# Two cross-attention layers in one launch: an own plan for the first seven steps, image tokens in five pieces, ScalarE's projection copies between layer 1's two pairs, image probabilities turned one place later

## The chip, the cores and the metric

The kernel runs on one core of one Trainium2 chip. What is measured is the device time of one execution in microseconds (us). The core has a matrix engine (TensorE, PE in the profile; its weight loads are the row PEld), a vector engine (VectorE, DVE), a scalar engine (ScalarE, ACT), a general engine (GpSimd, POOL) and a sync engine (SP) that issues transfers. Each engine works through its own list of instructions in the order in which the program issued them; semaphores hold an instruction until what it needs is there. Matrix products land in PSUM, and the other engines copy them from there to SBUF.

## What is computed

Eight batch entries of 256 rows and 320 channels go through two attention layers of 20 heads with 16 channels each. Both layers take their keys and values from 256 context tokens of 512 channels. Layer 0 treats the first 77 tokens as text and the other 179 as image tokens, with a softmax for each part. Layer 1 treats 252 as text and the last 4 as image tokens, and adds a term to the image scores: how alike the text context that a row attends to is to each image token.

```python
# layer 0
q = heads(x @ Wq.T); k, v from text; k_ip, v_ip from the rest
out = (softmax(q k / 4) v + softmax(q k_ip / 4) v_ip) @ Wo.T + bo + x
# layer 1, on layer 0's result
probs_t = softmax(q k_t / 4);  text_out = probs_t v_t
qsem = l2norm(probs_t @ text_ehs);  sem = qsem . l2norm(ip_ehs)
probs_ip = softmax(q k_ip / 4 + 0.5 * sem) * spatial_mask
out = (text_out + probs_ip v_ip) @ W_out + b_out + x
```

All numbers are float32. The biases are drawn small and not zero.

## The kernel before

**Steps.** The 20 heads of a batch entry are handled in five groups of four (QUADS), so a layer takes 40 steps. The loop at L910 walks n from 0: step n does group s = n % 5 of entry b = n // 5 for layer 0, and beside it the group of layer 1 that lies six steps back (SHIFT). The first six steps have no layer 1 in them, 34 steps have both layers, and at the end six steps have layer 1 alone; four more only drain. Nothing is reordered by a scheduler: manual_schedule keeps PE, DVE, ACT and POOL in the order in which the Python code issues the instructions.

**One step of both layers** (both_layers, L853). Scores of layer 0 go to four PSUM tiles (one for each head, held once each, so the next scores wait until these are emptied). DVE takes the row maxima (l0_max, L411, which run at L414), ACT the exponentials with their sums (l0_exp, L422, at L426), in two pairs of heads. PE turns each pair (transposed_probs, L349, at L357) into the same PSUM tiles, DVE and ACT copy the turned probabilities out (L362), and at the end of the step PE multiplies them with the values (l0_values, at L444). Between, layer 1 does the same: scores at L319, maxima and exponentials in max_exp1 (L849, at L614 and L626), the turning at L357, and, one step later, the products y with values and gram matrix (l1_values, L650 and L653), which DVE reduces (L657, L661). POOL prepares the masked queries sc_qz (L308) that the scores of either layer wait for.

**Fillers.** Everything else is put into seven places (0 to 6) of a step by a table in fillers (L778): projections to q, k and v of both layers (l0_q, l0_k, l0_v, l1_q, l1_k, l1_v), the gram matrix (l1_gram), output projections, layer 1's end (l1_norm to l1_out). A filler of this kind takes one of two PSUM tiles (mm_tile, L92), PE writes it, and ACT or DVE copies it out: ACT at L258 (q), L390 (k of layer 0), L399 and L401 (v of layer 0), L501 and L502 (k of layer 1), L536 (gram), L554 and L555 (v of layer 1). A third filler can't begin on PE before the first one's copy has been made. One place in the plan brings l1_k at place 4 (0, 4) and l1_xT at place 5 (0, 5), which turns layer 0's result for layer 1 (L287, with two such tiles). l1_probs_T (L708) turns layer 1's image probabilities on PE (L712), scales the text part on POOL (L721) and copies on DVE (L729); it stands in place 3 of group 3, ahead of layer 1's scores. l1_attn uses it in place 5.

**The first steps.** Steps 0 to 3 (n < NQ - 1) have a plan of their own; steps 4 to 6 use the general one. image_tokens (L209) prepares the 32 image tokens of all entries at once, at place 4 of step 1: turning them (L213, copied at L216), their keys (ps_kip, 24 products at L220), their values (L281, copied at L230), the squares on ACT (L233), their root on ACT (L235, with a table load, since the exponential's table must give way), the scaling on DVE (L236, L237), and turning the scaled tokens (L240, L243). Their source ip_sb comes by eight small transfers that POOL issues behind three weights (load_late, L759). encT and xT of entry 1 are issued on ACT's queue at step 2.

Of the kernel before, what the change touches and what calls it, by code (L numbers as in the profile page):

```python
# [50 lines left out]
def kernel(  # L51
# [40 lines left out]
    def mm_tile(name):  # L92
        return ps_mm.tile([P, 512], F32, tag="mm", name=name)
# [115 lines left out]
    def image_tokens(_):  # L209
        ipT = work.tile([P, NE, NB], F32, tag="aT", name="ipT", bufs=2)  # L210
        ps = mm_tile("ps_ipT")
        for k in range(NE):
            nc.tensor.transpose(  # L213
                ps[:, k * NB : (k + 1) * NB], ip_sb[:, k * P : (k + 1) * P], ident[:NB, :NB]
            )
        nc.vector.tensor_copy(ipT.rearrange("p k n -> p (k n)"), ps[:, : NE * NB])  # L216
        ps = mm_tile("ps_kip")
        for m in range(NC):
            for k in range(NE):
                nc.tensor.matmul(  # L220
                    ps[:, m * NB : (m + 1) * NB],
                    columns(wkip1, k, m),
                    ipT[:, k, :],
                    start=(k == 0),
                    stop=(k == NE - 1),
                )
        nc.vector.tensor_copy(kipA.rearrange("p m n -> p (m n)"), ps[:, : NC * NB])
        ps = mm_tile("ps_vip")
        project_rows(ps[:NB, :C], lambda k: ipT[:, k, :], wvip1)
        nc.vector.tensor_copy(vipA, ps[:NB, :C])  # L230
        sq = work.tile([NB, E], F32, tag="et1", name="ip_sq", bufs=2)
        rn = small.tile([NB, 1], F32, tag="ip_rn", name="ip_rn", bufs=1)
        nc.scalar.activation(sq, ip_sb, AF.Square, accum_out=rn)  # L233
        nc.vector.tensor_scalar_max(rn, rn, EPS2)
        nc.scalar.activation(rn, rn, AF.Sqrt)  # L235
        nc.vector.reciprocal(rn, rn)  # L236
        nc.vector.tensor_scalar_mul(sq, ip_sb, rn)  # L237
        ps = mm_tile("ps_ip")
        for k in range(NE):
            nc.tensor.transpose(  # L240
                ps[:, k * NB : (k + 1) * NB], sq[:, k * P : (k + 1) * P], ident[:NB, :NB]
            )
        nc.vector.tensor_copy(ipnT.rearrange("p k n -> p (k n)"), ps[:, : NE * NB])  # L243


    def project_q(dst, src, w, ms, name):
# [531 lines left out]
    def fillers(n, place):  # L778
# [45 lines left out]
        for f, at, *args in plan.get((s, place), ()):  # L824
            if 0 <= at < B:
                f(at, *args)
# [19 lines left out]

        return l1_begin(*divmod(n - SHIFT, NQ), 1 if n < N0 else n % 2)

    def max_exp1(u, x):  # L849
        l1_max(u, x)  # L850
        l1_exp(u, x)

    def both_layers(n, u, v1):  # L853

        u0 = l0_begin(*divmod(n, NQ))
        for pair in range(2):
            l0_max(u0, pair)
        l0_exp(u0, 0)
        fillers(n, 0)
        part(l1_values, v1, 0)  # L860
        l0_exp(u0, 1)
        fillers(n, 1)
        part(l0_attn, u)
# [12 lines left out]
        part(l1_values, v1, 3, (0,))  # L876
        part(l1_transposed, u1, 0)
        fillers(n, 5)
        part(l1_values, v1, 3, (1,))
        part(l1_transposed, u1, 1)  # L880
        fillers(n, 6)
        l0_values(u0)
        return u0, u1

    def layer_1(n, u, v1):

        fillers(n, 0)
        fillers(n, 1)
        part(l0_attn, u)
        u1 = begin1(n)  # L890
        part(max_exp1, u1, 0)
        part(l1_values, v1, 0)
        fillers(n, 2)
        part(max_exp1, u1, 1)
# [86 lines left out]
```

## Time and profile before

Three executions were timed, 943.75, 944.04 and 948.78 us, so the median is 944.04. The execution that was profiled took 944.11 us.

| | us |
|---|---|
| profiled execution | 944.11 |
| its span in the trace | 942.4 |
| outside the span | 1.7 |
| PE busy | 893.2 (95%) |
| PEld busy | 715.4 (76%) |
| DVE busy | 626.4 (66%) |
| ACT busy | 530.8 (56%) |
| POOL busy | 199.3 (21%) |
| mean granted TensorE clock | 0.987 |

A step begins with its scores of layer 0 (L319 on PE). Read so, the first seven steps lie as follows. The columns are the stretch, its length, PE's busy time in it and the mean granted clock of PE.

| step | from, to (us) | length | PE busy | clock |
|---|---|---|---|---|
| 0 | 13.80 to 25.01 | 11.21 | 11.21 | 1.00 |
| 1 | 25.01 to 46.16 | 21.15 | 17.23 | 0.84 |
| 2 | 46.16 to 59.04 | 12.88 | 12.88 | 0.87 |
| 3 | 59.04 to 72.46 | 13.42 | 12.48 | 1.00 |
| 4 | 72.46 to 85.80 | 13.34 | 10.83 | 0.87 |
| 5 | 85.80 to 105.44 | 19.64 | 17.55 | 1.00 |
| 6 | 105.44 to 122.63 | 17.19 | 15.81 | 1.00 |

In a timeline a row gives the start, the time from the first instruction's start to the last one's end, the engine, the line, the operation and the tiles, how many instructions are merged, and in brackets the idle time ahead of it with what ended it. A matmul's row overlaps the next by some 0.1 us. In the table of waits a row names who waited, for whom, how long in total, how often, and the longest.

### The profile page before, as it was taken

How to read it: one execution, taken by the hardware profiler on the slowest of the kernel's cores; microseconds unless marked ns; L12 is line 12 of the kernel's file. 1: busy time of each engine (PE TensorE's matmuls, PEld its weight loads, DVE VectorE, ACT ScalarE, POOL GpSimd, SP SyncE). 2: the span in 40 equal slices, each digit the busy share in tenths (PEclk: the TensorE clock that was granted, in tenths of full speed). 3: DMA queues.
4: the chain of work that ended last, by engine and by line, in shares of the span. 5: the costliest groups of instructions: out<-in, count | busy, mean ns of one | idle time of the engine just before them, and what ended most of it. 6: DMA issues, size and time to landing. Idle time of an engine off the chain costs nothing.

```text
span 942.4 us, 18840 instructions
## 1 busy us (share of the span) xinstructions
PE 893.2 (95%) x6296; PEld 715.4 (76%) x6296; DVE 626.4 (66%) x2127; ACT 530.8 (56%) x2314; POOL 199.3 (21%) x336
## 2 busy tenths in 40 slices
PE   7898999999999999999999999999999999899895
PEld 5576687878877787878787788777877787768773
DVE  2344466767776677766777667766777667875774
ACT  3476465746645576545666467555665556643650
POOL 5422221123121222122121221312221122212100
PEclk9899999999999999999999999999999999999997
DMA  8310010001000010000100001000100100000000
GB/s 267 99 46 1 15 41 1 1 15 36 9 2 15 16 44 2 15 16 23 23 1 15 15 24 22 2 15 15 44 2 8 26 2 1 1 15 1 1 15 15
DMA packets 16848, 21.89 MB, mean 23 GB/s; under 512 B 1632, under 2 KB 15904, under 8 KB 16752
## 3 DMA queue, kind: packets, MB, share of 16 engines
q1 hardware_dynamic: 12048, 12.49, 5.1%
q0 software_dynamic: 1296, 4.25, 1.5%
q10 hardware_dynamic: 3408, 3.95, 1.3%
q8 instruction: 51, 0.84, 0.4%
q14 instruction: 45, 0.37, 0.1%
HBM read 17.24 MB, written 2.62 MB: 21 GB/s over the span
## 4 chain that ended last, share of the span: by engine, by line
PE 66%; issue 15%; ACT 9%; DVE 5%; POOL 3%; DMA 1%; ACTq 0%; POOLq 0%; DVEq 0%
PE y L650 11%; PE sc L357 10%; PE sc L319 8%; PE v L281 6%; PE k L269 6%; PE p_o L294 6%; PE y L653 6%; PE q L251 5%; ACT e L626 5%; PE oT L444 4%; ACT e L426 4%; DVE nmx L614 2%; POOL sc_qz L308 2%; PE g L527 2%; PE p_aT_ps L287 1%
## 5 line engine op out<-in xcount | busy, mean ns | idle before, releaser
L426 ACT ACTIVATE e<-sc,nmx 128x77 f32<-128x77 f32 (+1 forms) x640 | 228.0, 416 | 58.2 <-DVE nmx L414 58.2
L626 ACT ACTIVATE e<-sc,nmx 128x252 f32<-128x252 f32 x320 | 145.8, 479 | 124.3 <-DVE aip L617 120.7
L650 PE MATMUL y<-gv,et 126*128 126x272 f32 x640 | 201.6, 396 | 3.8 <-DVE num L661 3.7
L357 PE MATMUL sc<-ident,e 128*126 128x128 f32 (+1 forms) x1280 | 171.3, 275 | 12.8 <-ACT e L426 7.3
L657 DVE CUSTOM_DVE_ANT_0 e<-y,e 128x252 f32<-128x252 f32 x320 | 133.6, 418 | 71.6 <-PE y L653 69.2
L414 DVE TENSOR_REDUCE nmx<-sc 128x2 f32<-128x154 f32 x320 | 109.7, 415 | 102.0 <-PE sc L319 102.0
L362 DVE COPY et<-sc 128x512 f32<-128x512 f32 (+1 forms) x228 | 151.2, 687 | 17.2 <-PE sc L357 14.4
L426 ACT ACTIVATION_READ_ACCUMULATOR e<-sc,nmx 128x1 f32 x640 | 162.2, 254 | 0.0
L357 PEld LDWEIGHTS sc<-ident,e 128*126 128x126 f32 (+1 forms) x1280 | 145.3, 141 | 22.0 <-ACT e L426 10.6
L653 PEld LDWEIGHTS y<-gv,et 126*128 126x128 f32 x640 | 120.8, 189 | 25.8
L653 PE MATMUL y<-gv,et 126*128 126x146 f32 x640 | 131.4, 287 | 0.0
L614 DVE TENSOR_REDUCE nmx<-sc 128x2 f32<-128x504 f32 x160 | 106.8, 675 | 29.3 <-PE sc L319 29.3
L650 PEld LDWEIGHTS y<-gv,et 126*128 126x128 f32 x640 | 104.4, 190 | 18.0 <-issue 4.7
L362 ACT COPY et<-sc 128x512 f32<-128x512 f32 (+1 forms) x92 | 53.2, 585 | 100.8 <-PE sc L357 100.8
L319 PE MATMUL sc<-k,sc_qz 32*128 32x256 f32 x1280 | 94.1, 404 | 2.9 <-POOL sc_qz L308 2.6
L479 POOL TENSOR_TENSOR attn<-o_sb 128x64 f32<-128x64 f32 x80 | 24.0, 321 | 313.3 <-DVE o_sb L469 310.3
L319 PEld LDWEIGHTS sc<-k,sc_qz 32*128 32x128 f32 x1280 | 58.9, 185 | 32.5 <-issue 21.7
L540 POOL COPY gv<-gv 126x3402 f32<-126x3402 f32 (+1 forms) x16 | 33.2, 2077 | 214.3 <-ACT gv L536 162.3
L308 POOL TENSOR_SCALAR sc_qz<-q,quad_m 128x256 f32<-128x256 f32 x80 | 73.2, 925 | 4.2 <-ACT q L258 4.2
L269 PE MATMUL k<-encT,wk 128*128 128x77 f32 (+1 forms) x384 | 72.8, 332 | 0.7 <-DMA wk<-in_WkT_dram 0.7
L269 PEld LDWEIGHTS k<-encT,wk 128*128 128x128 f32 x384 | 58.1, 190 | 16.3 <-issue 12.6
L626 ACT ACTIVATION_READ_ACCUMULATOR e<-sc,nmx 128x1 f32 x320 | 68.4, 214 | 0.0
(129 smaller groups left out, 1070.7 us busy)
## 6 DMA issues: line engine op xcount, KB each, us to landing
encT<-in_encT_dram SPq DMA_DIRECT2D x7, 512.0 KB
x<-in_x_dram SPq DMA_DIRECT2D x8, 320.0 KB
out_dram<-osb SPq DMA_DIRECT2D x16, 160.0 KB
xT<-in_xT_dram SPq DMA_DIRECT2D x7, 256.0 KB
xT<-in_xT_dram SPq DMA_DIRECT2D x7, 128.0 KB
vip_rows<-vipA SPq DMA_DIRECT2D x32, 25.0 KB
wk<-in_WkT_dram ACTq DMA_DIRECT2D x1, 640.0 KB
wkip<-in_WkipT_dram ACTq DMA_DIRECT2D x1, 640.0 KB
```

The costliest lines, as they stand in the source:

```text
L269: nc.tensor.matmul(ps[:, t0:t1], columns(w, k, m), encT_b[:, k, t0:t1], start=(k == 0), stop=(k == NE - 1),)
L308: nc.gpsimd.tensor_scalar_mul(qz, qT[:, m, :], quad_m[:, i : i + 1])
L319: nc.tensor.matmul(sc[j][:, half, :], qz[rows, half * P : (half + 1) * P], kT(j)[rows, m, :], start=True, stop=True,)
L357: nc.tensor.transpose(v[:, c, half, :], u["e"][x][:, j, half, t0 + c * tn : t0 + (c + 1) * tn], ident,)
L362: copies[j](u["et"][x][:tn, j].rearrange("p c n s -> p (c n s)"), ps)
L414: nc.vector.tensor_reduce(u["nmx"][x][:, j, :, a], u["sc"][2 * x + j][:, :, t0:t1], AX.X, ALU.max, negate=True,)
L426: nc.scalar.activation(u["e"][x][:, j, half, t0:t1], u["sc"][2 * x + j][:, half, t0:t1], AF.Exp, bias=u["nmx"][x][:, j, half, a : a + 1], ...
L614: nc.vector.tensor_reduce(u["nmx"][x][:, j, :], sc[:, :, t0 : t0 + TXT1], AX.X, ALU.max, negate=True)
L626: nc.scalar.activation(u["e"][x][:, j, half, t0 : t0 + TXT1], u["sc"][2 * x + j][:, half, t0 : t0 + TXT1], AF.Exp, bias=u["nmx"][x][:, j, ...
L650: nc.tensor.matmul(y, et[:, 1 - odd, half, :], gv[0][:, g, full], start=True, stop=False)
L653: nc.tensor.matmul(y[:, into], et[:, odd, half, :], gv[1][:, g, part], start=False, stop=True)
L657: nc.vector.tensor_tensor_reduce(e, y[:, g0 : g0 + TXT1], e, op0=ALU.mult, op1=ALU.add, scale=1.0, scalar=0.0, accum_out=r["n2"][:, half, ...
```

## The change

Four edits. image_tokens becomes five fillers: ip_squares (the squares and their sum, now one DVE instruction), ip_norm (root on ACT, reciprocal and scaling on DVE), ip_T (turning tokens and scaled tokens together), ip_k and ip_v. They stand in steps 1 and 2. The first seven steps (0 to 6) get one plan of their own; it issues the same fillers as those steps did before, at other places, each keyed by step and place. In both_layers the maxima of both pairs of layer 1 are issued first, then the exponentials of pair 0, then the fillers of place 4, and then the exponentials of pair 1; ACT's copies of place 4 so stand ahead of pair 1's exponentials, where they stood behind them. l1_probs_T moves from place 3 of group 3 to place 4, behind layer 1's scores and ahead of l0_q. In layer_1 max_exp1 is written out, with no change of order.

```diff
+    def ip_squares(_):
+        ip["n"] = work.tile([NB, E], F32, tag="et1", name="ip_n", bufs=2)
+        ip["rn"] = small.tile([NB, 1], F32, tag="ip_rn", name="ip_rn", bufs=1)
+        nc.vector.tensor_tensor_reduce(
+            ip["n"], ip_sb, ip_sb, op0=ALU.mult, op1=ALU.add,
+            scale=1.0, scalar=0.0, accum_out=ip["rn"],
+        )
+        nc.vector.tensor_scalar_max(ip["rn"], ip["rn"], EPS2)
+
+    def ip_norm(_):
+        nc.scalar.activation(ip["rn"], ip["rn"], AF.Sqrt)
+        nc.vector.reciprocal(ip["rn"], ip["rn"])
+        nc.vector.tensor_scalar_mul(ip["n"], ip_sb, ip["rn"])
...
-        nc.scalar.activation(sq, ip_sb, AF.Square, accum_out=rn)
...
-            (3, 3): [(l1_probs_T, old)],
-            (3, 4): [(l0_q, ahead, (0, 1))],
+            (3, 4): [(l1_probs_T, old), (l0_q, ahead, (0, 1))],
...
-        if n < NQ - 1:
-            plan = {
-                (0, 0): [(l0_v, 0, 0)],
-                (0, 1): [(l0_v, 0, 1)],
-                (0, 2): [(l0_v, 0, 2)],
-                (1, 0): [(l0_k, 0, 1)],
-                (1, 1): [(l0_q, 0, (2,))],
-                (1, 4): [(image_tokens, 0)],
-                (2, 0): [(l1_gram, 0, 0)],
-                (2, 1): [(l1_v, 0, 0)],
-                (2, 2): [(l0_k, 0, 2)],
-                (3, 0): [(l1_v, 0, 1)],
-                (3, 1): [(l0_v, 1, 0)],
-                (3, 4): [(l0_q, 1, (0, 1)), (l1_gram, 0, 1), (l1_image, 0)],
-            }
+        if n <= NQ + 1:
+            plan = (
+                {
+                    0: [(l0_v, 0, 0)],
+                    1: [(l0_v, 0, 1)],
+                    2: [(l0_v, 0, 2)],
+                },
+                {
+                    0: [(l0_k, 0, 1)],
+                    1: [(l0_k, 0, 2), (ip_squares, 0)],
+                    2: [(l0_q, 0, (2,)), (ip_norm, 0)],
+                },
+                {
+                    0: [(ip_T, 0), (ip_k, 0)],
+                    1: [(ip_v, 0)],
+                    2: [(l1_gram, 0, 0)],
+                    3: [(l1_v, 0, 0)],
+                },
+                {
+                    0: [(l1_v, 0, 1)],
+                    1: [(l0_q, 1, (0, 1)), (l1_image, 0)],
+                    2: [(l0_v, 1, 0)],
+                },
+                {
+                    0: [(l0_k, 1, 0)],
+                    1: [(l0_v, 1, 1)],
+                    2: [(l1_gram, 0, 1), (l1_k, 0, 0)],
+                },
+                {
+                    0: [(l0_v, 1, 2)],
+                    1: [(l0_k, 1, 1)],
+                    2: [(l0_q, 1, (2,)), (l0_attn_T, 0, 0)],
+                    3: [(l0_attn_T, 0, 1), (l0_out, 0, 0), (l0_out, 0, 1)],
+                    5: [(l1_xT, 0)],
+                    6: [(l1_q, 0, (0, 1))],
+                },
+                {
+                    0: [(l1_k, 0, 2)],
+                    4: [(l1_k, 0, 1)],
+                    5: [(l1_gram, 1, 0)],
+                },
+            )[n]
+            plan = {(s, at): f for at, f in plan.items()}
...
         u1 = begin1(n)
-        part(max_exp1, u1, 0)
-        part(max_exp1, u1, 1)
+        for pair in range(2):
+            part(l1_max, u1, pair)
+        part(l1_exp, u1, 0)
         fillers(n, 4)
+        part(l1_exp, u1, 1)
         part(l1_values, v1, 3, (0,))
         part(l1_transposed, u1, 0)
```

More of the change, by code (lines that the diff above doesn't have):

```diff
@@ L207, with ip_T, ip_k @@
     vipA = const.tile([NB, C], F32, tag="vipA", name="vipA")
-    def image_tokens(_):
-        ipT = work.tile([P, NE, NB], F32, tag="aT", name="ipT", bufs=2)
-        ps = mm_tile("ps_ipT")
-        for k in range(NE):
-            nc.tensor.transpose(
-                ps[:, k * NB : (k + 1) * NB], ip_sb[:, k * P : (k + 1) * P], ident[:NB, :NB]
+    ip = {}
+    def ip_squares(_):
[10 more added lines that the diff above has]
+        nc.vector.tensor_scalar_mul(ip["n"], ip_sb, ip["rn"])
+    def ip_T(_):
+        ip["T"] = work.tile([P, NE, NB], F32, tag="aT", name="ipT", bufs=2)
+        ps = mm_tile("ps_ipT")
+        for i, src in enumerate((ip_sb, ip["n"])):
+            for k in range(NE):
+                nc.tensor.transpose(
+                    ps[:, (i * NE + k) * NB : (i * NE + k + 1) * NB],
+                    src[:, k * P : (k + 1) * P],
+                    ident[:NB, :NB],
+                )
+        for i, dst in enumerate((ip["T"], ipnT)):
+            nc.vector.tensor_copy(
+                dst.rearrange("p k n -> p (k n)"), ps[:, i * NE * NB : (i + 1) * NE * NB]
             )
-        nc.vector.tensor_copy(ipT.rearrange("p k n -> p (k n)"), ps[:, : NE * NB])
+    def ip_k(_):
         ps = mm_tile("ps_kip")
@@ L222, in image_tokens @@
                     columns(wkip1, k, m),
-                    ipT[:, k, :],
+                    ip["T"][:, k, :],
                     start=(k == 0),
@@ L227, in image_tokens, with ip_v @@
         nc.vector.tensor_copy(kipA.rearrange("p m n -> p (m n)"), ps[:, : NC * NB])
+    def ip_v(_):
         ps = mm_tile("ps_vip")
-        project_rows(ps[:NB, :C], lambda k: ipT[:, k, :], wvip1)
+        project_rows(ps[:NB, :C], lambda k: ip["T"][:, k, :], wvip1)
         nc.vector.tensor_copy(vipA, ps[:NB, :C])
-        sq = work.tile([NB, E], F32, tag="et1", name="ip_sq", bufs=2)
-        rn = small.tile([NB, 1], F32, tag="ip_rn", name="ip_rn", bufs=1)
-        nc.scalar.activation(sq, ip_sb, AF.Square, accum_out=rn)
[L234 to L243, printed above, removed]
     def project_q(dst, src, w, ms, name):
@@ L847, in begin1 @@
         return l1_begin(*divmod(n - SHIFT, NQ), 1 if n < N0 else n % 2)
-    def max_exp1(u, x):
-        l1_max(u, x)
-        l1_exp(u, x)
     def both_layers(n, u, v1):
@@ L890, in layer_1 @@
         u1 = begin1(n)
-        part(max_exp1, u1, 0)
+        part(l1_max, u1, 0)
+        part(l1_exp, u1, 0)
         part(l1_values, v1, 0)
         fillers(n, 2)
-        part(max_exp1, u1, 1)
+        part(l1_max, u1, 1)
+        part(l1_exp, u1, 1)
         part(l1_values, v1, 1)
```

## The prediction

> **What bounds the kernel now.** I read the page's slices first, then the table of who waits for whom on PE in the steady part, the chain of waits there, and last the start in one-microsecond windows.
>
> ```profile
> PE   7898999999999999999999999999999999899895
> ...
> PEclk9899999999999999999999999999999999999997
> ```
>
> PE is busy nearly everywhere. Only two things can be won: PE's idle time, and time at a lower granted clock. Both lie in the first five slices (118 us) and at the very end. The steady part, 150 to 800 us:
>
> ```profile
> PE x1T_ps L287 <- ACT k L502: 7.5, 6, 1.3
> PE sc L357 <- ACT e L626: 2.7, 12, 0.3
> PE sc L319 <- POOL sc_qz L308: 2.0, 6, 0.6
> PE ipo L735 <- ACT q L258: 1.1, 5, 0.2
> ```
>
> Here the largest wait is one place, six times 1.25 us. The chain shows its cause:
>
> ```profile
> 419.86 1.58 ACT e L626 x7
> 421.44 0.26 ACT k L501
> 421.70 0.18 ACT k L502
> 421.87 0.04 issue
> 421.92 0.55 PE x1T_ps L287 x3
> ```
>
> PE had made this k by 418.57; its copies stood behind pair 1's exponentials on ACT, and x1T's second half needs its PSUM tile. The start, in PE's timeline and windows (window, length, PE, PEld, DVE, ACT, POOL, clock):
>
> ```profile
> 33.08 0.66 PE L357 MATMUL sc<-ident,e 128*128 128x128 f32 x4 [0.74 <-ACT e L426]
> ...
> 34.57 4.09 PE L220 MATMUL ps_kip<-ipT,wkip 128*128 128x32 f32 x24 [0.47 <-DVE ipT L216]
> 38.59 4.37 PE L281 MATMUL ps_vip<-wvip,ipT 128*32 128x320 f32 x8
> 44.83 0.41 PE L240 MATMUL ps_ip<-ident,ip_sq 32*128 32x32 f32 x4 [1.87 <-DVE ip_sq L237]
> ```
>
> ```profile
> 35.00:36.00 1.00, 1.00 (x11) 1.00 (x10) 0.00 (x0) 0.98 (x2) 1.00 (x4) 0.95 0.00 0
> 36.00:37.00 1.00, 1.00 (x7) 1.00 (x6) 0.00 (x0) 0.33 (x1) 0.64 (x1) 0.50 0.00 0
> ...
> 46.00:47.00 1.00, 1.00 (x15) 0.77 (x12) 0.00 (x0) 0.37 (x1) 0.00 (x0) 0.57 0.47 46
> ```
>
> The image tokens run at half clock, one after the other, with PE idle between. Steps 1 to 6 hold 10.8 us of PE idle (length less busy in the table of steps) and 6.8 us of lost clock (21.15 x 0.16 + 12.88 x 0.13 + 13.34 x 0.13): 17.6 us is all that the start could give.
>
> [...] half clock from 35.9 to 42.7, 46.1 to 49.5 and 80.3 to 83.7, lengths 6.8, 3.4 and 3.4, starts 10.24 (three windows) and 34.1 (ten) apart. [...] windows with PE 39 to 45% busy were enough (76.9 to 80.3: two turnings of 0.66), one with 66% (29.1 to 32.5) was not[...]. [...] the trace shows 1.28 and, with the next instruction 0.02 later (49.12 to 50.42), no drain. I use 1.28.
>
> **Part 1, ACT's copies between the pairs.** At group 0: pair 0's four exponentials end at 419.51, k's copies (0.46) end by 419.97, before x1T's second half is due at 420.50: the 1.25 goes. Pair 1's exponentials (four times 0.447) then end at 421.76 and not 421.29. What is late next: turning pair 1, which now comes up at 421.76, its second head at 422.2: no wait; then q of layer 1 at 422.6, with DVE's second x1T copy done by 422.2. So all six give 1.25: **7.5 us**. The seventh, in step 5, belongs to part 3. Behind a copy that waits for PE stand pair 1's exponentials: at group 3, q ends on PE 0.3 after pair 0's, its copy takes 0.5, pair 1 ends at 487.1 and is turned after 488.3. At groups 1, 2 and 4 the copies are 0.45, 0.26 and 0.43, and pair 1 ends some 1.1 before PE comes. These cost nothing while that margin stands. Bounds of the part: 6 to 8.5.
>
> **Part 2, image probabilities later.** At group 3 the scores wait 0.29 for POOL's sc_qz (released by the gram copy before it), and the turning (0.22 on PE's path) hides in that wait. Moved behind the scores it costs 0.22, five times; ACT's earlier copy of q removes ipo's 0.23, five times. DVE's copy of pT (0.41) moves into an idle 0.78 before y's. POOL's two scalings keep their order; none of SP's transfers moves. Sum 0, bounds -1.5 to 1.5. The last of them (step 38) falls into a wait of 1.0 and is free.
>
> **Part 3, the first seven steps.** They issue the same PE work, so only idle and clock can change. Starts of next rows give, at full clock: scores 1.08, k 2.21, q one group 1.30, two 2.6, v 2.2, o 0.22, turning a pair 0.87, values 1.00, gram 1.70 and 0.95, v of layer 1 2.28, k of layer 1 1.75. Exponentials begin 2.03 after the scores and take 2.76 for each pair.
>
> Step 1: exponentials end at 32.82 as before. Then ACT: k 0.25, q 0.48, table 1.28, root 0.20, to 35.03. On DVE the reciprocal waits for that root, and the third copy of turned probabilities is queued behind reciprocal and scaling: 35.03 + 0.15 + 0.05 + 0.70 (its row with the gap before it) + 0.69 = 36.6. Values wait for it on PE, which is idle from 34.0. Step 2 starts at 37.4. The square on DVE is not in the trace: 128x252 of its kind takes 0.42, so 512 elements 0.7 to 0.9; ip_sb's last issue is at 23.2 and the slowest landing 6.1, so it is done by 30.7 and hidden in DVE's idle time ahead of 35.
>
> Step 2: scores to 38.5, ip_T to 39.2. Its copy is queued behind DVE's eight maxima (2.74 from 38.6): ps_kip can start at 41.65, PE idle 2.4. Then 2.3 (11 in the full-clock us), 2.2, 0.22, 0.87, 1.70, 0.87, 2.28, 1.00: 53.1. POOL: the gram copy (3.03) now stands ahead of sc_qz (0.92), from 49.2: 0.5 late, 53.6. The exponentials' table load (1.28) and ACT's three transfer issues are hidden by ps_kip and ps_vip. The clock: two gaps of 2.6 and 2.4, then the narrow products, make half clock likely. It costs 1.8 (4.09 against 2.3) plus 2.1 (4.37 against 2.2) = 3.9 if it takes both, 0 if windows fall well. I take all: step 3 starts at 57.5, before 59.04: **gain 1.5**, bounds 0.5 (1 more in scores and values) to 5.4.
>
> Step 3: 1.08 + 2.28 + 2.6 + 0.22 + 0.87 + 2.2 + 0.87, the last turned head's copy on ACT 0.6, and what of the values must follow it 0.65: 11.4, before 13.42: gain 2.0. Step 4: 1.08 + 2.21 + 2.2 + 0.22 + 0.87 + 0.95 + 1.75 + 0.87 + 1.2 (the same copy and values) = 11.35 against 13.34: 2.0; POOL's sc_qz, behind gram and two k copies, is ready at 10.9. Step 5: 1.08 + 2.2 + 2.21 + 0.22 + 0.87 + 1.3, wait 0.2, turnings 0.33 + 0.87 + 0.33, output 3.24, then x1T without k in front: DVE's additions and copies are waited for 1.2 in all; 0.7 + 2.8 + 1.0: 18.45 against 19.64: 1.2. Step 6 loses k of layer 0 from its front, but there ACT sets the pace: exponentials end at 8.0 with two k copies between, scores of layer 1 end at 9.95; then 1.75, 0.3, 0.87, 1.70, 0.87, 1.6: 17.1. PE is idle 4 of 6 us, so half a window's clock goes too: 1.1. 18.2 against 17.19: **loss 1.0**.
>
> Sum of the start: 1.5 + 2.0 + 2.0 + 1.2 - 1.0 = 5.7. The profiled 944.1, which is the median within 0.1, less 7.5 and 5.7: **931 us**. The end of the kernel, with its 5.8 us wait, is untouched.
>
> **Rivals.**
> A, the start goes at full clock: 3.9 and 1.1 come back, 926. [...] Against: both gaps are over 2.4 of 3.4.
> B, the start gives nothing: the clock drops once more in steps 3 to 6 or step 2 lasts longer, only 7.5 remains: 944.1 - 7.5 = 936.6. For it: the clock took 6.8 us from these steps before, and nothing in the new plan keeps PE above half busy where it waits for DVE. Against: steps 3 to 5 lose 5.2 us of waits that have no part in it.
> C, the edit does not do what it says: the wait at x1T only moves to pair 1's turning or its copies on DVE. The start's 5.7 alone, 938.4. Against: 421.76 meets 421.76, with 0.4 for the second head.
> D, the delayed exponentials become PE's wait in all 34 steps: ACT's 0.45 to 0.65 exposed each time. It decides from 13.2 / 34 = 0.39 a step; at 0.65 it is 22 against 13.2: 953. Against: the margins of 1.1.
>
> **Chances.** Forecast 0.58, A 0.15, B 0.17, C 0.06, D 0.04. A measurement of this kernel tells 0.5% (4.7 us, 939.3) from no change. Faster: forecast, A, B and half of C, 0.92; same: the rest of C and some of D, 0.04; slower 0.04. The range takes in A and most of B and C: 925 to 938.
>
> **What would show it.** Right: no wait of x1T for k in the steady part, pair 1's turning without new waits; step 1 ending near 37.4 with PE waiting for DVE's copy behind the reciprocal; ps_kip waiting about 2.4 for ipT; half clock over ps_kip and ps_vip; steps 3 and 4 near 11.4. Wrong: L357 waiting for L626 by more than 3 us in the steady part, a step 2 with full clock, or a second drop in steps 3 to 5.

## The result and the profile after

Four executions of the changed kernel took 931.52 to 934.11 us, median **933.21**; four of the kernel before, beside them, 943.75 to 948.78, median 943.9. The ratio is 0.9872 [0.9837, 0.9907]: 1.3% less time. The execution that was profiled took 934.11 (span 932.4, mean clock 0.985). The forecast was 931 (925 to 938). The total is close, but it came about in another way than was worked out: the steady part gave more than was forecast, and the start gave nothing. That the two errors nearly cancel is luck.

Lines of the new kernel.py are numbered differently: L319 is now L332 (scores), L357 L370 (turnings), L362 L375 (copies of what was turned), L426 L439 and L626 L639 (exponentials of layers 0 and 1), L444 L457 (values), L287 L300 (x1T and other turnings), L735 L748 (ipo), L712 L725 (pT), L308 L321 (sc_qz). The slices of the page, of the kernel after:

```profile
PE   7899899999999999999999999999999999899895
...
PEclk9989899999999999999999999999999999999998
```

A slice is 23.3 us. In the second row two slices of the start stand at 8, the third and the fifth, where it was one: the start has lost more clock than before, not less (the amounts follow below). Now the steady part, who waits for whom on PE between 150 and 790 us (total, number, longest):

```profile
PE sc L332 <- POOL sc_qz L321: 3.0, 6, 0.6
PE sc L370 <- ACT e L639: 2.9, 13, 0.2
```

The 7.5 of x1T and the 1.1 of ipo are gone. What grew instead is small: pair 1's exponentials, now behind ACT's copies, are waited for 2.9 in 640 us. Before it was:

```profile
PE sc L357 <- ACT e L626: 2.2, 10, 0.3
```

The chain of waits through group 0 (start, length, what) shows nothing but PE:

```profile
417.67 0.89 PE sc L370 x8
418.56 0.65 PE x1T_ps L300 x6
419.21 0.46 PE y L663 x2
419.68 0.25 PE y L666 x2
419.92 0.88 PE sc L370 x8
420.80 2.59 PE q L264 x12
```

Before, x1T was two runs of three instructions with ACT's exponentials and k's copies between; now all six run as one.

The start, in PE's timeline of the kernel after:

```profile
36.62 1.06 PE L457 MATMUL oT<-et,v 128*32 128x256 f32 x12 [2.03 <-DVE et L375]
37.60 1.15 PE L332 MATMUL sc<-k,sc_qz 32*128 32x256 f32 x16
...
41.76 5.05 PE L244 MATMUL ps_kip<-ipT,wkip 128*128 128x32 f32 x24 [2.57 <-DVE ipT L236]
46.74 4.48 PE L294 MATMUL ps_vip<-wvip,ipT 128*32 128x320 f32 x8
...
59.41 1.15 PE L332 MATMUL sc<-k,sc_qz 32*128 32x256 f32 x16 [0.64 <-POOL sc_qz L321]
```

The two gaps ahead of the image tokens' keys lie where they were forecast (2.03 and 2.57), and both products run at half clock. Only the second gap lies in the 3.4 us ahead of the drop: from 38.7 to 42.1 PE was busy 25%, in the 3.4 us before that 60%. Further on, step 6:

```profile
108.28 0.66 PE L370 MATMUL sc<-ident,e 128*128 128x128 f32 x4 [0.74 <-ACT e L439]
110.11 0.91 PE L370 MATMUL sc<-ident,e 128*128 128x128 f32 x4 [1.17 <-ACT e L439]
111.50 1.11 PE L370 MATMUL sc<-ident,e 128*128 128x128 f32 x4 [0.48 <-ACT e L439]
112.54 3.15 PE L332 MATMUL sc<-k,sc_qz 32*128 32x256 f32 x16
115.62 3.73 PE L282 MATMUL k<-encT,wk 128*128 128x252 f32 x8
```

The same scores take 1.15 and the same k 1.97 at full clock. The windows of PE's clock give the extent (window, length, PE, PEld, DVE, ACT, POOL, clock, DMA share, GB/s):

```profile
42.00:43.00 1.00, 1.00 (x7) 1.00 (x7) 0.00 (x0) 1.00 (x8) 0.00 (x0) 0.55 0.16 50
43.00:46.00 3.00, 3.00 (x16) 3.00 (x16) 0.00 (x0) 3.00 (x20) 0.00 (x0) 0.50 0.01 3
...
110.00:111.00 1.00, 0.89 (x4) 0.51 (x4) 0.00 (x0) 1.00 (x8) 0.39 (x3) 0.68 0.00 0
111.00:120.00 9.00, 8.52 (x34) 6.02 (x33) 3.43 (x9) 3.56 (x15) 0.00 (x0) 0.50 0.00 1
```

The clock reads 1.00 from 41 to 42 and 0.50 from 43 to 46, so 0.55 between them means 0.9 of that microsecond at half clock. So half clock lasts from 42.1 to 52.3 and from 110.4 to 120.6: 10.24 us each time. The shortest stretch in the trace of before lasted 3.41 (46.1 to 49.5); it is called a window here, and 10.24 is three of them.

All runs were read in the same way, by the starts of the scores of layer 0. Steps 0 to 6 are the start, 7 to 39 the steady part, and the rest is what comes ahead of step 0 and behind step 39's end (one profiled execution of each kernel, us):

| kernel | step 1 | 2 | 3 | 4 | 5 | 6 | start, 0 to 6 | steady | rest | span |
|---|---|---|---|---|---|---|---|---|---|---|
| before | 21.15 | 12.88 | 13.42 | 13.34 | 19.64 | 17.19 | 108.83 | 717.00 | 116.6 | 942.4 |
| after | 12.39 | 21.81 | 11.95 | 13.02 | 18.91 | 21.11 | 110.40 | 706.10 | 115.9 | 932.4 |
| e1_copies | 22.46 | 12.73 | 13.41 | 13.48 | 19.64 | 17.17 | 110.10 | 705.41 | 115.9 | 931.4 |
| e2_probsT | 20.81 | 13.03 | 13.41 | 13.49 | 19.63 | 20.16 | 111.74 | 716.67 | 117.3 | 945.7 |
| e3_start | 13.14 | 22.75 | 11.95 | 13.02 | 18.91 | 21.10 | 112.08 | 716.38 | 115.7 | 944.2 |
| e4_kback | 12.50 | 21.83 | 11.94 | 13.04 | 17.90 | 17.47 | 105.89 | 706.40 | 117.4 | 929.7 |
| e5_filled | 12.53 | 16.93 | 11.94 | 13.04 | 18.93 | 17.63 | 102.21 | 706.39 | 116.4 | 925.0 |
| e6_norm | 12.01 | 20.19 | 11.94 | 13.03 | 18.93 | 20.14 | 107.45 | 706.39 | 117.1 | 930.9 |
| e7_best | 11.39 | 15.98 | 11.94 | 12.20 | 17.89 | 17.17 | 97.77 | 705.39 | 117.2 | 920.4 |
| e8_tail | 12.02 | 19.05 | 11.95 | 12.21 | 17.91 | 20.17 | 104.52 | 705.59 | 113.8 | 923.9 |
| e9_oldfill | 17.87 | 12.69 | 13.42 | 11.81 | 19.64 | 17.19 | 103.83 | 705.66 | 116.0 | 925.5 |
| e10_full | 11.71 | 16.07 | 11.95 | 12.21 | 17.91 | 17.19 | 98.25 | 705.61 | 113.9 | 917.8 |

From before to after the steady part gave 10.9 us, the start took 1.6, and the rest gave 0.7: together 10.0, the difference of the spans. The 0.7 is no effect of the change that could be told from chance: in the runs whose end is the same program the rest lies between 115.7 and 117.4. The starts scatter too: e2_probsT has the start of the kernel before and took 2.9 longer there. A single start is therefore never read without its clock.

### The profile page after: what moved, and what is told of

Same layout as the page of the kernel before. It is cut to its first block, busy times and chain, and to the rows that moved or that the text cites. A ratio compares the mean times of both kernels' runs of the same rounds, so it can differ in the third digit from the quotient of the medians.

```text
span 932.4 us, 18776 instructions
## 1 busy us (share of the span) xinstructions
PE 892.6 (96%) x6296; PEld 718.9 (77%) x6296; DVE 624.2 (67%) x2129; ACT 529.9 (57%) x2312; POOL 198.9 (21%) x336
## 4 chain that ended last, share of the span: by engine, by line
PE 74%; issue 13%; ACT 4%; DVE 4%; POOL 3%; DMA 1%; ACTq 0%; SPq 0%; POOLq 0%; DVEq 0%
PE y L663 12%; PE sc L370 11%; PE sc L332 8%; PE k L282 8%; PE v L294 7%; PE q L264 6%; PE y L666 6%; PE p_o L307 6%; PE oT L457 4%; ACT e L439 3%; POOL sc_qz L321 2%; PE g L540 1%; PE p_aT_ps L300 1%; DVE nmx L627 1%; PE ipo L748 1%
## 5 line engine op out<-in xcount | busy, mean ns | idle before, releaser
L439 ACT ACTIVATE e<-sc,nmx 128x77 f32<-128x77 f32 (+1 forms) x640 | 227.3, 415 | 58.7 <-DVE nmx L427 58.7
L639 ACT ACTIVATE e<-sc,nmx 128x252 f32<-128x252 f32 x320 | 146.9, 482 | 124.4 <-DVE aip L630 118.6
L370 PE MATMUL sc<-ident,e 128*126 128x128 f32 (+1 forms) x1280 | 171.1, 276 | 8.1 <-ACT e L639 5.3
L375 DVE COPY et<-sc 128x512 f32<-128x512 f32 (+1 forms) x228 | 150.8, 686 | 23.5 <-PE sc L370 21.0
L439 ACT ACTIVATION_READ_ACCUMULATOR e<-sc,nmx 128x1 f32 x640 | 162.1, 254 | 0.0
L370 PEld LDWEIGHTS sc<-ident,e 128*126 128x126 f32 (+1 forms) x1280 | 146.9, 142 | 15.9 <-ACT e L639 9.4
L375 ACT COPY et<-sc 128x512 f32<-128x512 f32 (+1 forms) x92 | 53.1, 584 | 90.1 <-PE sc L370 90.1
L332 PE MATMUL sc<-k,sc_qz 32*128 32x256 f32 x1280 | 94.3, 404 | 4.4 <-POOL sc_qz L321 4.2
L332 PEld LDWEIGHTS sc<-k,sc_qz 32*128 32x128 f32 x1280 | 59.1, 185 | 34.1 <-issue 21.5
L282 PE MATMUL k<-encT,wk 128*128 128x77 f32 (+1 forms) x384 | 75.0, 339 | 0.9 <-ACT v L412 0.9
L321 POOL TENSOR_SCALAR sc_qz<-q,quad_m 128x256 f32<-128x256 f32 x80 | 73.0, 923 | 4.2 <-ACT q L271 4.2
L282 PEld LDWEIGHTS k<-encT,wk 128*128 128x128 f32 x384 | 59.6, 195 | 17.5 <-issue 12.4
L639 ACT ACTIVATION_READ_ACCUMULATOR e<-sc,nmx 128x1 f32 x320 | 69.6, 217 | 0.0
```

Of the source, the lines that this page charges most:

```text
L282: nc.tensor.matmul(ps[:, t0:t1], columns(w, k, m), encT_b[:, k, t0:t1], start=(k == 0), stop=(k == NE - 1),)
L321: nc.gpsimd.tensor_scalar_mul(qz, qT[:, m, :], quad_m[:, i : i + 1])
L332: nc.tensor.matmul(sc[j][:, half, :], qz[rows, half * P : (half + 1) * P], kT(j)[rows, m, :], start=True, stop=True,)
L370: nc.tensor.transpose(v[:, c, half, :], u["e"][x][:, j, half, t0 + c * tn : t0 + (c + 1) * tn], ident,)
L375: copies[j](u["et"][x][:tn, j].rearrange("p c n s -> p (c n s)"), ps)
L439: nc.scalar.activation(u["e"][x][:, j, half, t0:t1], u["sc"][2 * x + j][:, half, t0:t1], AF.Exp, bias=u["nmx"][x][:, j, half, a : a + 1], ...
```

## Experiments: which of the three edits carries the gain

My theory after the result: ScalarE's copies carry all of it, the new start carries nothing since the clock takes what the waits give, and the later image probabilities cost a little. The rival is the forecast's split, some 7.5 from the copies and 5.7 from the start. Three kernels each have one edit alone; the image tokens' pieces and the plan of the first steps count as one here.

**e1_copies: only the copies between the pairs**, on the kernel before.

```diff
-        part(max_exp1, u1, 0)
-        part(max_exp1, u1, 1)
+        for pair in range(2):
+            part(l1_max, u1, pair)
+        part(l1_exp, u1, 0)
         fillers(n, 4)
+        part(l1_exp, u1, 1)
```

> The kernel before with one edit alone: layer 1's two maxima first, pair 0's exponentials, the fillers of place 4, pair 1's exponentials. Theory (the gain is made here, in the steady part): x1T's wait for k goes at six groups, 1.48 us each (1.25 on PE's row, 1.48 on its weight loads), and ipo's wait for q at five groups, 0.5 each: 943.9 - 8.9 - 2.5 = 932.5. Rival (the prediction's own term): 1.25 each and ipo 0.23: 943.9 - 7.5 - 1.2 = 935.2. Rival (the gain is the start plan's): 943.

Measured: 933.3 us (932.7 to 934.84), ratio 0.9878 [0.9851, 0.9904] to the kernel before on the same chip (945.52): all of the gain of the whole change, from one edit of a few lines. VectorE's order stays as it was; only the place of ScalarE's copies changes. Its steady part is 11.6 shorter. Group 0 went from 26.71 to 25.23 us, group 3 from 20.80 to 20.29; groups 1, 2 and 4 stayed within 0.1, on the mean. Its waits on PE between 150 and 790 us:

```profile
PE sc L357 <- ACT e L626: 2.9, 13, 0.2
PE sc L319 <- POOL sc_qz L308: 1.9, 6, 0.6
```

**e2_probsT: only the image probabilities, one place later.**

```diff
-            (3, 3): [(l1_probs_T, old)],
-            (3, 4): [(l0_q, ahead, (0, 1))],
+            (3, 4): [(l1_probs_T, old), (l0_q, ahead, (0, 1))],
```

> The kernel before with one edit alone: the turning of the image probabilities goes from place 3 to place 4, behind layer 1's scores. Theory: the scores wait for POOL's sc_qz anyway, so the turning loses its cover, 0.25 us at five groups, and nothing is won, since q's copy still stands behind all exponentials: group 3 takes 20.8 to 21.1 us where it took 20.80, the whole 944 to 945.5. Rival (the turning and its DVE copy delayed the maxima): group 3 shorter by 0.3, the whole 942.5.

Measured: one execution, 947.41 us; the 15 of the kernel before on that chip lie between 941.76 and 949.08, so the time tells nothing. The groups do: group 3 took 20.77 against 20.80. Beside the copies the same edit costs 0.15 in five groups (20.44 in the kernel after, 20.29 in e1). The forecast's zero stands within its bounds. The scores' wait for sc_qz was to cover the turning, and it grew instead: 3.0 in all where it was 2.0.

**e3_start: only the start**, that is the whole change without the two edits above (max_exp1 is back, and the probabilities stand at place 3).

> The changed kernel with the two steady edits undone: the new plan of steps 0 to 6 with the image tokens in five pieces, alone. Theory from the two traces: the plan wins in steps 1, 3, 4 and 5 and gives it back at half clock in steps 2 and 6, 1.6 us slower over steps 0 to 6: 943.9 + 1.6 = 945.5, within 2 as the clock's windows fall. Prediction on record: 943.9 - 5.7 = 938.2. Rival (the plan is what gains): below 936.

Measured: 945.93 us (12 executions, 943.53 to 947.72), ratio 1.0002 [0.9987, 1.0017] to 15 of the kernel before. The new plan alone is worth nothing that can be measured. Its profiled start took 112.08 against 108.83.

So the copies carry the gain, and the rival's split falls. Why the start gives nothing is the next question.

## Experiments: what the start lost, and to whom

The waits were forecast one by one. Did they go? PE's idle time in each step (length less busy), and the clock:

| step | before: idle, clock | after: idle, clock |
|---|---|---|
| 1 | 3.92, 0.84 | 2.03, 1.00 |
| 2 | 0, 0.87 | 3.20, 0.77 |
| 3 | 0.94, 1.00 | 0, 1.00 |
| 4 | 2.51, 0.87 | 0.90, 1.00 |
| 5 | 2.09, 1.00 | 1.28, 1.00 |
| 6 | 1.38, 1.00 | 2.72, 0.76 |
| sum idle | 10.8 | 10.1 |
| lost clock | 6.8 | 21.81 x 0.23 + 21.11 x 0.24 = 10.1 |

The plan moved the waits from steps 1, 3, 4 and 5 to steps 2 and 6 and took away 0.7 us in all. The clock took 3.3 more. (The two make 2.6 where 1.6 was measured; a stretch that is idle at half clock is counted in both, and the rest I leave open.) So the clock did not take what the waits gave, as my theory has it: the waits gave little to begin with, and the clock took more than that. If waiting is what brings half clock, it must go when the waits are filled, whatever they are filled with.

**e5_filled: fifteen needless products** of 128x256 in the waits of steps 1, 2 and 6 of the kernel after. Nothing reads their results.

```diff
+    def dummy(_, count):
+        spare = ps_y.tile([P, S], F32, tag="y", name=f"spare_{count}")
+        for i in range(count):
+            nc.tensor.matmul(
+                spare, ident, bat[0]["encT"][:, i % NE, :], start=True, stop=True
+            )
...
+                    6: [(dummy, 0, 4)],
...
-                    0: [(ip_T, 0), (ip_k, 0)],
+                    0: [(ip_T, 0), (dummy, 0, 5), (ip_k, 0)],
...
+                    1: [(dummy, 0, 4)],
+                    2: [(dummy, 0, 2)],
```

> The changed kernel with needless products of 128x256 (0.43 us each by the q projection's rows) added where PE was idle in the first steps: 4 ahead of the values of step 1, 5 between ip_T and ip_k in step 2, 4 and 2 around the turnings of step 6; their result is not used. Theory (idle gaps of 2 to 2.6 us pull the clock down for whole windows of 3.4 us): the added work, 6.5 us of it, lies in the gaps, the clock stays full, ps_kip falls from 5.05 to 2.3 and ps_vip from 4.48 to 2.2, step 2 from 21.8 to 16.7 and step 6 from 21.1 to 17.5; the whole 933.2 - 8 = 925. Rival (narrow products or the plan's waits are what is slow): steps 1, 2 and 6 keep their lengths or grow by the added work, 933 to 938.

Measured: 926.72 us, ratio 0.9820 [0.9799, 0.9841], some 0.5% less than the kernel after by the ratios, and the start 8.2 us shorter in the profiled executions. Three of the four executions have a mean clock of 0.994; the fourth, 930.5 us, has 0.991: it lost more clock, and no trace shows where. More work on the busiest engine made the kernel quicker. Its timeline:

```profile
39.07 2.43 PE L794 MATMUL spare<-encT,ident 128*128 128x256 f32 x10
41.71 2.87 PE L244 MATMUL ps_kip<-ipT,wkip 128*128 128x32 f32 x24 [0.21 <-DVE ipT L236]
44.51 2.34 PE L294 MATMUL ps_vip<-wvip,ipT 128*32 128x320 f32 x8
```

ps_kip starts at the same time as in the kernel after (41.71 and 41.76), as it waits for the same copy on DVE; but it takes 2.87, not 5.05, and ps_vip 2.34, not 4.48. So in these two executions half clock went with the waiting ahead of these products; that they are narrow didn't bring it by itself.

**e4_kback: one projection back from step 5 to step 6**, where it stood before.

```diff
-                    1: [(l0_k, 1, 1)],
...
-                    0: [(l1_k, 0, 2)],
+                    0: [(l0_k, 1, 1)],
+                    1: [(l1_k, 0, 2)],
```

> The changed kernel with one filler moved back: k of layer 0 for entry 1, group 1, leaves step 5 and stands at place 0 of step 6, where it stood before, with k of layer 1 behind it at place 1. Theory (step 6 was starved of PE work, and the clock fell): step 5 falls by the 2.2 us of that filler to 16.7, step 6 goes from 21.1 to about 17.2 with no half clock: 933.2 - 6 = 927. Rival (step 6 is set by ACT and the clock falls anyway): step 6 stays at 20 to 21, only step 5's 2.2 is won: 931.

Measured: 930.32 us, ratio 0.9837 [0.9805, 0.9869]. Step 6 has no half clock in the profiled execution and takes 17.47, not 21.11, though it has 2.2 us more to do. In step 5 the exponentials are waited for again, 0.74 and 0.40, so taking the projection out saves only 1.0 there. The two steps together took 35.37, against 40.02 with k in step 5: the move cost 4.65 us between these two executions, and 3.3 by the ratios, whose intervals overlap. Part of this is chance. e7_best and e8_tail below have k back in step 6 too, and that step took 17.17 in one and 20.17, with half clock, in the other.

**e6_norm: the root one place later**, so that the copy of turned probabilities is no longer queued behind reciprocal and scaling on DVE.

```diff
-                    2: [(l0_q, 0, (2,)), (ip_norm, 0)],
+                    2: [(l0_q, 0, (2,))],
+                    3: [(ip_norm, 0)],
```

> The changed kernel with ip_norm (root on ACT with its table load, reciprocal and scaling on DVE) moved from place 2 to place 3 of step 1, behind the copies of the turned probabilities. Theory (the third and fourth of these copies stood behind the table load and the reciprocal): PE's wait of 2.0 ahead of the values goes to 0.4, step 1 from 12.4 to 10.7; step 2 keeps its wait for the copy of ip_T, so the clock may still fall there: 933.2 - 1.6 = 931.6. Rival (the wait moves to ip_T, which needs the scaled tokens): step 2 grows by what step 1 loses, 933.

Measured: 932.37 us, ratio 0.9870 [0.9855, 0.9884], the same as after. The wait of 2.03 went, and another was right behind it:

```profile
37.14 1.15 PE L332 MATMUL sc<-k,sc_qz 32*128 32x256 f32 x16 [1.41 <-POOL sc_qz L321]
```

POOL's masked queries for step 2 come only just before 37.1. Step 1 took 12.01, and half clock stayed. The forecast had named the right queue, but taking it away is worth 0.4.

**e7_best: the start mended by what had been seen.** Image probabilities back at place 3; the root at place 3; the gram matrix ahead of the image tokens' keys, so that PE has work while DVE copies; k of layer 1 ahead of the gram matrix in step 4; k of layer 0 back in step 6.

```diff
-                    0: [(ip_T, 0), (ip_k, 0)],
-                    1: [(ip_v, 0)],
-                    2: [(l1_gram, 0, 0)],
-                    3: [(l1_v, 0, 0)],
+                    0: [(ip_T, 0), (l1_gram, 0, 0)],
+                    1: [(ip_k, 0), (ip_v, 0)],
+                    2: [(l1_v, 0, 0)],
...
-                    2: [(l1_gram, 0, 1), (l1_k, 0, 0)],
+                    2: [(l1_k, 0, 0), (l1_gram, 0, 1)],
```

> What the runs so far point to, together: ACT's copies between the pairs kept, the image probabilities back at place 3, k of layer 0 back in step 6, ip_norm at place 3 of step 1, in step 2 the gram matrix between ip_T and ip_k (it fills the wait for the copy of ip_T, and takes POOL's gram copy away from the next step's queries), in step 4 k of layer 1 ahead of the gram matrix (its PSUM tile is free earlier). Theory: step 1 10.7, step 2 14.5 to 16, step 4 12.1, step 5 17.9, step 6 17.5, group 3 20.29 for 20.43: 933.2 less 1.7, 6, 0.9, 4.6 and 0.8 = 919. Rival (the clock falls at the narrow ps_kip whatever stands ahead): step 2 near 19, 923.

Measured: 923.34 us (922.11 to 927.0), ratio 0.9788 [0.9764, 0.9812], 0.85% less than the change as it stands (0.9788 / 0.9872). Step 2 takes 15.98 with ps_kip waiting 0.96. No step of the profiled execution is at half clock (1.00 from 25 to 112 us). But its four executions show mean clocks of 0.994, 0.994, 0.991 and 0.987, in the order of their times: the slower two lost more clock, and no trace shows where.

**e8_tail: the same question at the end of the kernel.** PE waits there 5.8 us for DVE ahead of the last turning. Twelve needless products go into that wait, on e7_best. The expectation also speaks of needless products in the first steps and of k copied by VectorE; this kernel has neither.

```diff
+        if (n, place) == (N0 + SHIFT + 2, 3):
+            dummy(B - 1, 12)
```

> The version that was quickest so far (ScalarE's copies between the pairs, the start's plan with k copied by VectorE, and the needless products in the first steps), with 12 further needless products of 128x256 ahead of the last turning, where TensorE waits 5.8 us for VectorE; their results are not used. If half clock is granted after idle stretches of TensorE and the last output stage pays for that one, the stage from the last turning to the end falls from 12.3 us by about 3.5 (ipo 2.50 to 1.24, aT 1.75 to about 0.8, p_o from 4.0 to 4.9 down to about 3.3), and the time from 923.3 to about 920. Rival: the last stage's clock has another cause, or the products hold up the last turning by what they save: 923 to 925, and ipo still 2.5.

Measured: 923.03 us (922.27 to 925.6), ratio 0.9756 [0.9728, 0.9783]; the median is 0.3 us below e7's, and the ratio, on another chip, 0.3% (some 3 us) below with intervals that overlap. So the times don't settle it. The last stage did what the theory said. First e7_best, then e8_tail:

```profile
906.63 0.65 PE L725 MATMUL pT<-ident,fus 128*80 128x128 f32 x2 [5.80 <-DVE fus L719]
907.79 2.50 PE L748 MATMUL ipo<-vip,pT_sb 80*128 80x320 f32 x4 [0.51 <-DVE pT_sb L742]
910.09 1.75 PE L300 MATMUL p_aT_ps<-ident,attn 128*128 128x128 f32 x6
911.63 5.39 PE L307 MATMUL p_o<-wo,p_aT 128*128 128x320 f32 x12
```

```profile
913.47 0.41 PE L725 MATMUL pT<-ident,fus 128*80 128x128 f32 x2 [0.28 <-DVE fus L719]
914.40 1.34 PE L748 MATMUL ipo<-vip,pT_sb 80*128 80x320 f32 x4 [0.51 <-DVE pT_sb L742]
915.85 1.07 PE L300 MATMUL p_aT_ps<-ident,attn 128*128 128x128 f32 x6
917.05 3.50 PE L307 MATMUL p_o<-wo,p_aT 128*128 128x320 f32 x12
```

The rest of the span fell from 117.2 to 113.8, by 3.4. In the profiled execution the start hid it: the same start took 97.77 in e7's and 104.52 in e8's. Of the 6.75 between them 0.6 is in step 1, where the scores behind it waited longer for POOL (1.41 for 0.78); the rest goes with the clock, with ps_kip at 3.98 for 2.84, ps_vip at 4.28 for 2.34 and half clock in step 6. In e7's trace the clock is 1.00 from 25 to 112 us; in e8's it is 0.50 from 43.0 to 49.8, and in step 6 scores take 2.73 for 1.92 and k 3.73 for 1.97. So some 6 us between two executions of one start go with the clock.

**e9_oldfill: the old start at full clock**, e1_copies with ten needless products in the waits of steps 1 and 4. The new start is worth nothing as it stands; is it worth something when neither pays for the clock?

```diff
+        dummy(0, 1)
         ps = mm_tile("ps_kip")
...
+        dummy(0, 4)
         ps = mm_tile("ps_ip")
...
+                (1, 2): [(dummy, 0, 2)],
                 (1, 4): [(image_tokens, 0)],
...
+        if (n, place) == (4, 2):
+            dummy(0, 3)
```

> The old plan of the start with ScalarE's copies between the pairs, and ten needless products of 128x256 in the waits of steps 1 and 4 (two ahead of pair 1's turning, one ahead of ps_kip, four ahead of the turning of the scaled tokens, three in step 4); their results are not used. It asks what the new plan is worth when neither start pays for the clock. Theory 1: the new plan saves almost no waiting (10.8 us idle before, 10.1 after), so the old one at full clock is as good as the new one with needless products (start 102.2, time 926.7): start 102 to 103.5, time 926 to 928. Theory 2: the new plan's shorter waits are worth the 3 to 4 us of steps 3 to 5 that the forecast gave it, and only the clock hid that: start 105 to 106, time 929 to 930. If half clock is still there, neither can be told.

Measured: 929.05 us (927.14 to 930.99), ratio 0.9823 [0.9788, 0.9857]. The profiled execution had no half clock in its start (1.00 from 25 to 118 us), and took 103.83 there, between the two theories and near the first. Against e5_filled's 102.21, one execution each, the new plan is worth some 1.6 us of waiting. Two of the four executions took 3.7 us longer, at a mean clock of 0.991, again with no trace that shows where. The old image tokens, one after the other, are hardly worse once nothing runs at half clock:

```profile
34.70 2.84 PE L228 MATMUL ps_kip<-ipT,wkip 128*128 128x32 f32 x24
37.47 2.34 PE L290 MATMUL ps_vip<-wvip,ipT 128*32 128x320 f32 x8
39.74 1.99 PE L212 MATMUL spare<-encT,ident 128*128 128x256 f32 x8
```

**e10_full: e8_tail with seven needless products in the start**, meant to leave no 3.4 us of it in which PE mostly waits.

```diff
                     3: [(ip_norm, 0)],
+                    6: [(dummy, 0, 2, "a")],
...
-                    1: [(ip_k, 0), (ip_v, 0)],
+                    1: [(dummy, 0, 2, "b"), (ip_k, 0), (dummy, 0, 1, "c"), (ip_v, 0)],
...
                     1: [(l1_k, 0, 2)],
+                    2: [(dummy, 0, 2, "d")],
```

> The kernel with the needless products ahead of the last turning, and seven more in the first steps: two at the end of step 1, two ahead of ps_kip, one ahead of ps_vip, two in step 6; their results are not used. Without them the first seven steps took 97.8 us in one profiled execution and 104.5 in another, with half clock over ps_kip and ps_vip and in step 6 in the second. Theory: windows of the clock fall anew in each execution, and a start whose waits are filled never reaches half clock: start 98 to 99.5 in every execution, granted clock 0.996 or more, time 917 to 919. Rival: the needless products are too few or in the wrong place, and some executions still have half clock: clocks from 0.991 to 0.996 and 920 to 924.

Measured: **919.82 us** (919.51 to 921.62), ratio 0.9731 [0.9697, 0.9766]; mean clocks 1.0, 0.998, 1.0 and 1.0. The start took 98.25 in the profiled execution; that is 0.5 more than e7's best case, and no execution has e7's worst. The time is 0.8 above what was expected, the clock as expected. The slices:

```profile
PE   7999999999999999999999999999999999899898
...
PEclk9999999999999999999999999999999999999999
```

It is the quickest version of this study, 1.4% below the change as it stands (0.9731 / 0.9872).

## Why the forecast was near, and where its steps failed

**The sum.** 944.1 - 7.5 - 5.7 = 931 was the forecast; 944.1 - 10.9 + 1.6 - 0.7 = 934.1 was the profiled execution. The start failed by 7.3 one way, steady part and end by 4.1 the other. Rival B described what happened: "the start gives nothing: the clock drops once more in steps 3 to 6 or step 2 lasts longer". Both came. B's price of 936.6 missed the profiled 934.1 by the steady part's 3.4, the start's 1.6 and the end's 0.7: 936.6 - 3.4 + 1.6 - 0.7 = 934.1. It had 0.17. The 931 is near because two errors have opposite signs, which is luck; the mechanism of the copies was right, that of the start was not.

**Part 1, right in mechanism, under-sized.** The x1T wait went at all places, and no margin of exponentials failed (rivals C and D). But each group 0 gave 1.48, not 1.25. The 1.25 came from PE's row of the table of waits. The row of the weight loads for the same place, kernel before, 150 to 790 us, has the full price:

```profile
PEld x1T_ps L287 <- ACT k L502: 8.9, 6, 1.5
PEld ipo L735 <- ACT q L258: 3.7, 5, 0.7
```

8.9 / 6 = 1.48 is what the group lost. In an unbroken run the loads begin ahead of their products: x1T's first at 420.06, its product at 420.17, while the turning ahead ran until 420.33. Behind the wait load and product both begin at 421.92. That this makes up the 0.24 between the two rows there (1.49 and 1.25) is my guess; no run separates it. At ipo, too, more was won than PE's row says: its two pairs lay 1.57 apart from start to the next row (486.11 to 487.68), and 1.08 now (482.70 to 483.78). That is 0.5 for each of five groups, where I put 0.23 from PE's row (1.1 / 5). The weight loads' row has 0.74 there (3.7 / 5), so it is not the exact price either.

**Part 2, zero within its bounds.** The gain from ipo was 0.5, as said, but e1 has that without the move. The move itself costs 0.15: POOL sets when the scores begin, so their wait for it grew from 0.29 to 0.49 when the turning left it, and the turning now has no cover behind them. "The turning hides in that wait" was right of the place before.

**Part 3, the step that failed.** Step 1 was forecast to last 12.4 and took 12.39, with the wait at the copy behind the reciprocal. Step 2's waits were right (2.4 forecast, 2.57; 0.5 and 0.64), and half clock was taken in full over ps_kip and ps_vip. But step 2 took 21.81, not 20.1. I had priced ps_kip with its row of before, 4.09, of which the first 1.3 us (34.57 to 35.9) were at full clock; wholly at half clock it is 5.05. And half clock ended only at 52.3, so that ps_vip's 4.48 was followed by a slow o (0.69 for 0.38) and a slow turning (1.39 for 1.04): together the 1.7. Step 3 was 11.95 (11.4 forecast) and step 4 13.02 (11.35). In step 4 I had missed one wait:

```profile
79.82 1.97 PE L282 MATMUL k<-encT,wk 128*128 128x252 f32 x8 [0.90 <-ACT v L412]
```

k of layer 1 needs the PSUM tile that v of layer 0 holds until ACT has copied it. The rest is the end of a step: from the last turned pair's start to the next scores 2.75 us pass in step 4 (81.63 to 84.38), where I took 2.07 (0.87 and 1.2). With both, 11.35 becomes 12.93; and step 3's 11.4, with the second alone, 12.1. Step 5 took 18.91 (18.45; the terms as written come to 18.55). Step 6 was the largest miss: 21.11, forecast 18.2. Its idle time was seen ("PE is idle 4 of 6 us"), and then half a window was charged for it. It was three: the waits of 0.74 and 1.17 take 1.91 of the 3.41 us ahead of 110.4, and turnings, scores and k up to 120.6 pay. Without the move this step took 17.47 in e4 at full clock, and 20.17 in e8, where the clock fell all the same.

**What the forecast took of the clock.** The window of 29.1 to 32.5 had PE busy 71%, not 66%. The next, 32.5 to 35.9, ahead of the first drop, had it busy 69%: 1.3 us of ps_kip and 30% of other products. The forecast has the narrow products among what makes half clock likely. In e5_filled they fill 2.4 of the 3.4 us from 42.1 to 45.5, and the clock stayed full (2.87 and 2.34 above), though the other products alone are some 30% of that window, less than the 44% with which the clock fell at 110.4. (The place of this window is an estimate, counted back in steps of 3.413 from 919.3, where the last product's row, 4.66 for 3.50 at full clock, puts the end of half clock.)

**What was asked to be seen.** No x1T wait: seen. Step 1 near 37.4: 37.60. ps_kip waiting 2.4: 2.57. Half clock over ps_kip and ps_vip: seen. Steps 3 and 4 near 11.4: not so. A second drop in steps 3 to 5 was named as a sign of being wrong; it came in step 6.

## What to carry to other kernels

Moving an engine's copy ahead of work that nobody waits for yet can be worth a whole wait in every group, and costs only as long as that work had slack: read the slack where it will be needed, and read the wait on the weight loads' row too, since PE's own row gave too low a price at both places here. A plan for the start of a kernel is to be judged by how its waits lie together, not by their sum: one window of 3.4 us with PE mostly waiting (25% busy from 38.7 to 42.1) cost 5 us here, in the products behind it (10.24 us at half clock). Where such waits can't be removed, needless products in them can be the cheapest remedy (the start took 98.25 in e10_full, 104.52 in e8_tail), though in e5_filled and e9_oldfill some executions still lost clock; executions must be compared by their granted clock before a plan is called better or worse.

## What the runs showed of the hardware that was not expected

Half clock lasted three windows (10.24 us) twice in the start of the kernel after, though PE was busy 8.52 of 9.00 us in the second of these stretches. In the start of the kernel before it lasted two windows (35.9 to 42.7) and twice one (46.1 to 49.5, 80.3 to 83.7). With that same start in e1_copies it lasted at least 9.7 us: ps_kip, from 34.74, took 5.30, and ps_vip, to 44.45, took 4.48. With the new start in e4_kback all rows from 37.69 to some 51.0 are slow: scores 2.09 for 1.15, ps_kip 5.33, ps_vip 3.83 for 2.34. One window without idle time was not always enough to bring full clock back: in the kernel after PE was never idle from 113.8 to 117.2, and half clock lasted until 120.6. In the kernel before it was never idle from 46.1 to 49.5, and full clock followed. What brings the clock back sooner or later was not found and stays open.

Within each of the two traces the stretches of half clock begin a whole number of windows apart: in the kernel before at 35.9, 46.1, 80.3 and 926.8, that is 10.24, 34.13 and 846.5 us or 3, 10 and 248 times 3.413; in the kernel after at 42.1, 110.4 and 919.3, that is 68.27 and 808.96 us or 20 and 237 times. The place of the first is not tied to the program: with one and the same start the clock fell at 35.9 in the kernel before, and at 34.74 at the latest in e1_copies.

Waits that are each short were enough: 0.74 and 1.17 us within one window, between turnings of 0.66, came ahead of the drop at 110.4, with PE busy 1.50 of 3.41 us. With turnings alone in e1_copies PE was busy 55% from 30.8 to 34.2, and ps_kip behind them ran at half clock (5.30); it was busy 67% from 92.2 to 95.6, and the output product behind kept its 3.40 of full clock. But no share of busy time decided alone: in the kernel before the clock fell after 69% (32.5 to 35.9) and stayed full after 63% (199.7 to 203.2) and 59% (821.0 to 824.4), and in the kernel after it stayed full after 52% (912.5 to 915.9).

One and the same start took 97.77 and 104.52 us in two executions, and step 6 of the old plan 17.19 in one and 20.16 in another. The scatter of the kernel before goes with the clock in the same way: of 15 executions on one chip the quickest, 941.76, had a mean clock of 0.991 and the slowest, 949.08, 0.984. In e10_full, with the waits of start and end filled, four executions lay within 2.1 us; in e5_filled and e9_oldfill, where only the start is filled, they lay 3.9 apart.
